# A four-layer graph network on one core: 8 more node blocks gathered in the first pass, two weights joined, casts and one-hots on other engines, 40 instead of 36 blocks by weight matrix

## The chip, the cores and the metric

The kernel runs on one core of one Trainium2 chip. The metric is device time in microseconds: the median of the runs before the change is 8338.6 us (three runs, 8333.83 to 8340.75).

The core has five engines with a queue each, which work through their instructions in order: PE (matmuls; PEld is its loading of weights, which overlaps), DVE (vectors), ACT (scalar functions, copies, casts), POOL (general purpose; here it issues the gathers) and SP (issues most of the plain DMAs). SBUF is the memory on the chip, PSUM holds PE's results.

## The reference

Four layers over one graph of 12,500 nodes with 64 features and 212,500 directed edges (sorted by destination). Each adds its result to x and normalizes each row:

```python
msgs = x[src]                                              # layer 0, SAGE, twice
mean = segment_sum(msgs, dst) / maximum(deg, 1)
h = relu(mean @ Wl.T + bl + x @ Wr.T)
h = relu(h @ W1.T + b1) @ W2.T + b2
out = sage(h)                                              # conv2_Wl, conv2_bl, conv2_Wr
msg = silu(batchnorm(concat(x[row], edge_attr) @ W1 + b1)) # layer 1, summed by node
out = segment_sum((feat @ weight + h_bias)[src] * attention, dst)    # layer 2
for _ in range(3):                                         # layer 3
    h = segment_sum(norm[:, None] * h[src], dst)
```

## The kernel before

Nodes lie in 98 blocks of 128. Edges lie in 1664 groups of up to 128, 8 groups to a chunk (208 chunks). A sum over the edges of a node block is formed in one of two ways.

**Gathered** (`gather_pass`): for each group POOL fetches 128 source rows with one indirect DMA (line 382, tile `msg`), DVE makes a one-hot of the destinations (line 297, `oh` or `ohs`), and PE multiplies one with the other into the block's PSUM tile `ps` (line 334). A group touches one to three blocks. Precision comes from cutting f32 into three bf16 parts side by side (`split`, lines 279 to 285): ACT casts `hi`, DVE takes the rest, ACT casts `mid`, DVE takes `lo`. POOL, DVE, ACT and PE each come in turn.

**By matrix**: the block's rows of the adjacency matrix times all 98 blocks of sources, with no gathering.

The work runs in six stages:

1. *First pass* (about 190 to 1460 us of the profile). `adjacency` (line 586) builds the fp8 adjacency of blocks 28 to 97 from windows of 4 nodes: one-hots of keys (DVE, line 608) and sources (DVE, line 601), a product `pb` (PE, line 613), a cast to fp8 (ACT, line 617), and a write of each block to DRAM (`t_adj`, line 626). As each is finished, its product with the node features, `px` (line 790, 98 matmuls), is spread over the building of the next. Beside it the first 496 groups are gathered from `t_x` for blocks 0 to 29. Blocks 28 and 29 get a share of both, kept in `shares` and added. Each finished sum goes through `conv1` (line 715): mean, three 64-wide layers one after another (line 722), then a product with the second convolution's two weights (line 726), splits, and writes to `t_h` and `t_hs`. `together` deals the steps of the two sides evenly.
2. *Second pass* (to 2204 us): blocks 30 to 97 with `t_adj` read back in halves (`at`, line 354, 4 buffers; `pd`, line 359), the first 496 groups gathered from `t_h`.
3. *Edge rows* (2214 to 4300 us): all 1664 groups are gathered from `t_y`, added to the edges' own product (`pe`, lines 871 and 872), copied (`h`, line 874) and written with the one-hots to DRAM. Beside it `weight_matrix` (line 677) builds the attention-weighted adjacency of the last 36 blocks in f32: for each window of 4 nodes a `wkeys` one-hot (DVE, line 690), three weighted one-hots `wlows` (DVE, line 694, one for each bf16 part of the weights), three matmuls `pw` (line 697), a copy `aw` (ACT, line 698), and a write of four windows (SP, line 700).
4. *Silu sums* (4300 to 4840 us): per chunk, ACT applies silu to the rows read back (`z`, line 911), PE transposes (`pm`), `split_messages` makes the bf16 parts, and the stored one-hots are read for the product `ps`. Messages are made two chunks ahead. `update` follows for each block.
5. *Weighted sums* (4952 to 6301 us): the last 36 blocks by the stored f32 matrix (`by_matrix`, line 1036: 7 loads of 0.9 MB and 196 matmuls `pdw`, line 1044, per block), the others from 1064 groups gathered from `t_a`, scaled by ACT (line 1034). A `Later` queue delays the steps that follow a block (transposes, products, table writes) by so many pieces of the matrix.
6. *Three hops* (6331 us to the end), each like the second pass, over `t_g`.

In stages 1 to 4 and 6 a scheduler sets the order of instructions within each queue; in stage 5 it is the program's own order for ACT, DVE and PE.

Of the kernel before, what the change touches and what calls it, by code (L numbers as in the profile page):

```python
# [32 lines left out]

NW = 36
W = 128
# [24 lines left out]
def static_windows(n_nodes, n_edges):  # L60


    last = -(-n_nodes // P) * P - 1
    out = []
    for e, n in edge_groups(n_edges):
        margin = LEAST + int(MARGIN * 2 * (e * (n_edges - e)) ** 0.5 / n_edges)
        lo = e * n_nodes // n_edges - margin
        hi = (e + n) * n_nodes // n_edges + margin
        lo, hi = min(max(lo, 0), last), min(max(hi, 0), last)
        if n < P:  # L70
            hi = last
        out.append((lo // P, hi // P - lo // P + 1))
    return out


# [173 lines left out]
def fast(ctx: ExitStack, net: Net):  # L249
# [9 lines left out]
    bmax = max(b0 + n - 1 for b0, n in wins[:G0])  # L259
    dmin = min(b0 for b0, _ in wins[G0:])  # L260
    HB = NB // 2
    assert NB % 2 == 0 and G0 % J == 0 and dmin <= bmax + 1 and all(n <= 2 for _, n in wins[:G0])

# [14 lines left out]

    def split(parts, t, rest):

        hi, mid, lo = parts
        nc.scalar.copy(hi, t)
        nc.vector.tensor_tensor(rest, t, hi, ALU.subtract)  # L283
        nc.scalar.copy(mid, rest)  # L284
        nc.vector.tensor_tensor(lo, rest, mid, ALU.subtract)
# [111 lines left out]

    def split_messages(work, t, bufs=4):
# [3 lines left out]
        split(thirds(msg), t, rest)  # L402
        return msg
# [21 lines left out]

    def transposed(t):

        m = t.shape[1]
        pt = psum.tile([P, P], F32, name="pxt", tag="a")
        nc.tensor.transpose(pt[0:m, :], t, ident)  # L430
        xt = node.tile([P, P], F32, name="xt")
        nc.scalar.copy(xt[0:m, :], pt[0:m, :])
        return xt[0:m, :]
# [152 lines left out]
    def adjacency(block):  # L586
# [3 lines left out]
        with tc.tile_pool(name="build", bufs=1) as build:  # L590
            for b in range(dmin, NB):
                w0, w1 = b * P // D, min((b + 1) * P // D, n_win)
# [83 lines left out]

    def weight_matrix(kw, wkey, wlow, parts, ramps):

        kramp, lramp = ramps
        for b in range(B0, NB):  # L680
            w0 = b * PW
            for w in range(w0, w0 + PW, 4):
                n = max(0, min(4, n_win - w))
                aw = kw.tile([P, 7, 4, CS], F32, name="aw", bufs=3)
                if n < 4:
                    nc.vector.memset(aw, 0.0)
                for i in range(n):
                    k = w + i - QB * RW
                    keys = kw.tile([P, KEYS], BF16, name="wkeys", bufs=4)
# [14 lines left out]
                yield  # L704
# [8 lines left out]
    t_hs = dram.tile([P, NB, T3], BF16, name="t_hs")  # L713

    def conv1(b, ps):
        nc.vector.tensor_single_scalar(rdeg[:, b : b + 1], ps[:, T3 : T3 + 1], CU, ALU.max)
        nc.vector.reciprocal(rdeg[:, b : b + 1], rdeg[:, b : b + 1])  # L717
        nc.vector.tensor_single_scalar(dinv2[:, b : b + 1], ps[:, T3 : T3 + 1], CU, ALU.add)
        h = transposed(mean_and_own(b, ps))
        for weight, bias, func in ((net.w1, BL1, AF.Relu), (wt[:, M1, :], BM1, AF.Relu), (wt[:, M2, :], BM2, AF.Identity)):  # L720
            p1 = psum.tile([F, P], F32, name="p1", tag="a")
            nc.tensor.matmul(p1, weight, h, start=True, stop=True)  # L722
            h = node.tile([F, P], F32, name="h1")
            nc.scalar.activation(h, p1, func, bias=col[0:F, bias : bias + 1])
# [23 lines left out]
    with tc.tile_pool(name="xs0", bufs=1) as xp:  # L748
        xx = xp.tile([P, NB, XW], BF16, name="xx")
        with (  # L750
# [31 lines left out]


            shares = kl.tile([P, bmax - dmin + 1, T3 + 1], F32, name="shares")
            shared = set()

            def block(b, a):
                pd = psum.tile([P, T3 + 1], F32, name="px")
                for s in range(NB):
                    nc.tensor.matmul(pd, a[:, s, :], xx[:, s, 0 : T3 + 1], start=s == 0, stop=s == NB - 1)  # L790
                    if s % 7 == 6:
                        yield
                if b > bmax:
                    conv1(b, pd)
                else:
                    nc.scalar.copy(shares[:, b - dmin, :], pd)
                    shared.add(b)

            def gathered_block(b, ps):
                if b >= dmin:  # L800
                    assert b in shared
                    both = node.tile([P, T3 + 1], F32, name="both")
                    nc.vector.tensor_tensor(both, ps[:, 0 : T3 + 1], shares[:, b - dmin, :], ALU.add)
                    ps = both
                conv1(b, ps)
# [98 lines left out]
    with tc.tile_pool(name="keep1", bufs=1) as keep1, tc.tile_pool(name="work2s", bufs=2) as work:  # L904
        hT = keep1.tile([F, NP], F32, name="hT")

        def silu_message(c):
# [94 lines left out]

    GW = -(-(1 + max(g for g, (b0, _) in enumerate(wins) if b0 < B0)) // J) * J
    with tc.tile_pool(name="xs3", bufs=1) as xp:
        xs = xp.tile([P, NB, T3], BF16, name="xs")

        def weighted_sum(b, total):
# [13 lines left out]

            later3.add(3, columns)

        later3 = Later()

        with tc.tile_pool(name="work3", bufs=1) as work, tc.tile_pool(name="adj3", bufs=4) as adj:
# [10 lines left out]
            def by_matrix():  # L1037
                for b in range(B0, NB):
# [14 lines left out]
                    def to_rows(b=b, sums_t=sums_t):  # L1053
                        pt = psum.tile([P, F], F32, name="pxw", tag="c", bufs=2)
                        nc.tensor.transpose(pt, sums_t, i64)
                        weighted_sum(b, pt)

                    later3.add(2, to_rows)

# [442 lines left out]
```

## Time and profile before

| what | us |
|---|---|
| median of three runs | 8338.6 |
| the profiled execution | 8331.0 |
| its span, first to last instruction | 8329.2 |
| PE busy | 7023.3 (84%) |
| POOL busy | 5140.4 (62%) |
| DVE busy | 4699.4 (56%) |
| ACT busy | 3293.7 (40%) |

Busy shares are means over six stages with different limits, so each stage has to be read by itself. A profile line of a group gives the source line, the engine, the operation, output<-input, shapes and count, then its busy time, the mean length of one in ns, and the idle time before it with what ended it. A line of waits gives who waited for whom: us in total, times, longest. A line of the timeline gives start, length, engine, line, operation. "issue" is time in which an engine waited for nothing that the profile shows.

### The profile page before, as it was taken

The page shows a single profiled execution, that of the slowest core. Times are in us where ns is not written, and L with a number is a line of the kernel's source. Part 1 is how long each engine was busy: PE and PEld are TensorE (multiplying, and loading weights), DVE is VectorE, ACT ScalarE, POOL GpSimd, SP SyncE. Part 2 cuts the span into 40 slices and gives each one's busy share as a digit, 9 for nine tenths or more (in the row PEclk, how much of TensorE's full clock was granted, in tenths as well). Part 3 has the DMA queues.
Part 4 walks back from the last instruction along what each step waited for, and adds up shares of the span by engine and source line. Part 5 has one row for each costly group of instructions (what it writes and reads, how often), then busy time and mean ns, then how long its engine had stood idle before and what let it go on. Part 6 is the DMA issues. An engine that isn't in the chain of part 4 may idle for free.

```text
span 8329.2 us, 168327 instructions
## 1 busy us (share of the span) xinstructions
PE 7023.3 (84%) x63175; PEld 5984.5 (72%) x63176; DVE 4699.4 (56%) x16465; ACT 3293.7 (40%) x7517; POOL 5140.4 (62%) x5281
## 2 busy tenths in 40 slices
PE   1999999999866666666768877888889999999999
PEld 0777777899744444444447767777778999999999
DVE  7999998333478999998976642222222232322333
ACT  5888888111123333333348854444442111111110
POOL 4644442777477777777740017777776776776775
PEclk9999999899888888888879968999999999999999
DMA  4433333666567788877789946777776776776676
GB/s 103 137 114 120 122 113 113 196 206 197 173 218 246 250 257 261 262 252 247 251 268 328 327 152 243 250 254 263 267 268 215 217 217 211 217 217 213 211 219 183
DMA packets 863605, 1786.57 MB, mean 214 GB/s; under 512 B 250245, under 2 KB 511904, under 8 KB 853695
## 3 DMA queue, kind: packets, MB, share of 16 engines
q1 hardware_dynamic: 629944, 1382.63, 49.2%
q0 software_dynamic: 171856, 216.73, 11.1%
q10 hardware_dynamic: 60980, 176.35, 5.7%
q8 instruction: 501, 8.21, 0.4%
q14 instruction: 324, 2.65, 0.1%
HBM read 1217.67 MB, written 557.45 MB: 213 GB/s over the span
## 4 chain that ended last, share of the span: by engine, by line
PE 42%; POOL 24%; DMA 13%; issue 11%; DVE 6%; ACT 4%; POOLq 0%; ACTq 0%; DVEq 0%; SPq 0%
POOL msg L382 24%; PE pd L359 15%; DMA msg<-t_y,srci 8%; PE px L790 7%; PE pb L613 4%; PE ps L334 4%; DMA msg<-t_a,srci 3%; PE pw L697 3%; DMA msg<-t_g,srci 2%; PE p L722 1%; PE pe L872 1%; DVE rest L283 1%; ACT parts L284 1%; DVE junk L511 1%; PE ps L359 1%
## 5 line engine op out<-in xcount | busy, mean ns | idle before, releaser
L359 PEld LDWEIGHTS <-at 128*128 128x128 fp8e4 x27440 | 2280.0, 98 | 21.0 <-issue 15.5
L359 PE MATMUL pd<-xs,at 128*128 128x192 bf16 x26656 | 2264.5, 247 | 2.8 <-DMA at<-t_adj 2.8
L382 POOL DMA_INDIRECT msg<-t_y,srci x1664 | 1570.1, 944 | 582.1 <-issue 442.5
L382 POOL DMA_INDIRECT msg<-t_g,srci x1488 | 1406.8, 945 | 567.9 <-issue 453.8
L382 POOL DMA_INDIRECT msg<-t_a,srci x1064 | 1025.0, 963 | 985.8 <-DMA t_a<-xa 661.7
L697 PE MATMUL pw<-wkeys,wlows 128*128 128x392 bf16 x3423 | 1012.8, 389 | 172.8 <-ACT h L874 102.5
L694 DVE TENSOR_SCALAR wlows<-wramp,wlow,wpart 128x132 bf16<-128x132 f16 x3423 | 975.0, 334 | 231.8 <-PE pw L697 223.9
L378 DVE TENSOR_REDUCE sum<-pd 128x64 f32<-128x192 f32 x272 | 97.3, 358 | 1765.1 <-PE pd L362 1235.8
L698 ACT COPY aw<-pw 128x392 f32<-128x392 f32 x1141 | 554.6, 486 | 1224.2 <-PE pw L697 1209.0
L617 ACT ACTIVATE a<-pb 128x784 fp8e4<-128x784 f32 x1115 | 916.9, 825 | 156.2 <-PE pb L613 99.1
L382 POOL DMA_INDIRECT msg<-t_x,srci x496 | 563.8, 1137 | 608.1 <-PE pb L613 280.6
L1044 PE MATMUL pdw<-atw,xa 128*64 128x128 f32 x7056 | 879.5, 286 | 7.5 <-issue 7.5
L872 PE MATMUL pe<-ident,msg 128*128 128x128 f32 x1664 | 424.8, 344 | 508.2 <-DMA msg<-t_y,srci 505.8
L1044 PEld LDWEIGHTS pdw<-atw,xa 128*64 128x64 f32 x7056 | 822.6, 144 | 40.9 <-issue 32.7
L872 PEld LDWEIGHTS pe<-ident,msg 128*128 128x128 f32 x1664 | 337.2, 235 | 635.9 <-issue 463.5
L790 PE MATMUL px<-xx,a 128*128 128x193 bf16 x6860 | 779.0, 248 | 1.6 <-DVE rdeg L717 0.7
L297 DVE TENSOR_SCALAR oh<-ramp,drel 128x258 bf16<-128x258 f16 x2480 | 740.7, 338 | 6.5 <-PE ps L334 5.8
L697 PEld LDWEIGHTS <-wlows 128*128 128x128 bf16 x3423 | 382.8, 112 | 468.6 <-DVE wlows L694 371.4
L790 PEld LDWEIGHTS <-a 128*128 128x128 fp8e4 x6860 | 582.8, 98 | 159.9 <-issue 45.9
L608 DVE TENSOR_SCALAR keys<-line,key 128x392 bf16<-128x392 f16 x2229 | 625.6, 326 | 93.9 <-PE pb L613 83.6
L613 PE MATMUL pb<-keys,lows 128*128 128x392 bf16 x2229 | 571.2, 330 | 7.9 <-ACT a L617 3.4
L382 POOL DMA_INDIRECT msg<-t_h,srci x496 | 469.0, 945 | 169.4 <-issue 137.4
(233 smaller groups left out, 8978.0 us busy)
## 6 DMA issues: line engine op xcount, KB each, us to landing
at<-t_adj SPq DMA_DIRECT2D x560, 784.0 KB
t_w<-aw SPq DMA_DIRECT2D x288, 784.0 KB
atw<-t_w SPq DMA_DIRECT2D x252, 896.0 KB
ohs<-t_oh SPq DMA_DIRECT2D x279, 516.0 KB
t_adj<-a SPq DMA_DIRECT2D x70, 1568.0 KB
t_oh<-ohs ACTq DMA_DIRECT2D x176, 516.0 KB
ec<-in_ea SPq DMA_DIRECT2D x208, 256.0 KB
t_e<-h ACTq DMA_DIRECT2D x208, 256.0 KB
```

Of the source, the lines that this page charges most:

```text
L297: nc.vector.tensor_scalar(oh[:, 0 : 3 * ramp.shape[2]], ramp, net.drel[:, g : g + 1], one, ALU.is_equal, ALU.mult)
L359: nc.tensor.matmul(ps[:, 0:T3], at[:, s, :], xs[:, h * HB + s, :], start=start, stop=left == 0)
L382: nc.gpsimd.indirect_dma_start(out=out, out_offset=None, in_=table, in_offset=bass.IndirectOffsetOnAxis(ap=net.srci[:, g : g + 1], axis=0),)
L608: nc.vector.tensor_scalar(keys, net.line[:, 0:KEYS], key[:, w - Q0 * RW : w - Q0 * RW + 1], CU, ALU.is_equal, ALU.mult)
L613: nc.tensor.matmul(pb[:, i % 2, 0:KEYS], lows[:, i, :], keys, start=True, stop=True)
L617: nc.scalar.activation(a[:, :, at : at + k * D].rearrange("p s (k d) -> p k s d", d=D), pb[:, 0:k, 0:KEYS].rearrange("p k (s d) -> p k s d ...
L694: nc.vector.tensor_scalar(lows, lramp, wlow[:, k : k + 1], parts[j][:, k : k + 1], ALU.is_equal, ALU.mult)
L697: nc.tensor.matmul(pw, lows[:, 0:P], keys, start=j == 0, stop=j == 2)
L698: nc.scalar.copy(aw[:, :, i, :], pw.rearrange("p (a c) -> p a c", a=7))
L790: nc.tensor.matmul(pd, a[:, s, :], xx[:, s, 0 : T3 + 1], start=s == 0, stop=s == NB - 1)
L872: nc.tensor.matmul(pe[:, at], both, ident, start=False, stop=True)
L1044: nc.tensor.matmul(pd, xa[:, a * (NB // 7) + s, :], at[:, :, s * D : (s + 1) * D], start=a == 0 and s == 0, stop=a == 6 and s == NB // 7 - 1,)
```

## The change

- First pass: blocks 28 to 35 are now gathered whole (624 groups, `GA`, instead of 496; `below=BA` cuts off what falls into later blocks). `shares` goes. Their adjacency is still built, for the later passes, but with no `px`; the build order is 36, 37, 38, 39, 28, 40 to 45, 29, and so on, one of the eight after every six.
- The MLP's last weight has no nonlinearity behind it: `join_weights` multiplies it once with the next convolution's two weights (`m2lr`), and its bias likewise (`blr`, on all partitions). `conv1` has two 64-wide layers, one product, and one add `rr`.
- Second pass: 5 buffers of `at` instead of 4. `aw`, `wkeys` and `wlows` move from the pool `kw`, open in stages 2 and 3, to the pool of stage 3.
- Weight matrix: 40 blocks instead of 36. DVE makes the one-hot for part 0 as before and a bare one (`low1`); ACT makes those of parts 1 and 2 by scaling it.
- Silu sums: the cast of `mid` is a copy on POOL instead of ACT.
- Weighted sums: 1000 groups gathered; delays of 4 in two places (3 and 2 before); two PSUM tags exchanged.

```diff
-NW = 36
+NW = 40
...
+def chunks_below(wins, b):
+
+    return -(-(1 + max(g for g, (b0, _) in enumerate(wins) if b0 < b)) // J) * J
...
+    BA = dmin + J
+    GA = chunks_below(wins, BA)
+    build_order = []
+    for b in range(BA, NB):
+        build_order.append(b)
+        if b - BA >= 3 and (b - BA - 3) % 6 == 0 and dmin + (b - BA - 3) // 6 < BA:
+            build_order.append(dmin + (b - BA - 3) // 6)
...
-    def split(parts, t, rest):
+    def split(parts, t, rest, second=nc.scalar.copy):
...
-        nc.scalar.copy(mid, rest)
+        second(mid, rest)
...
-    def transposed(t):
+    def transposed(t, tag="a", bufs=None):
...
-            for b in range(dmin, NB):
+            for b in build_order:
...
                     pw = psum.tile([P, KEYS], F32, name="pw", tag="agg", bufs=3)
+                    low1 = work.tile([P, 132], BF16, name="wlow1", bufs=4)
+                    nc.vector.tensor_single_scalar(low1, lramp, wlow[:, k : k + 1], ALU.is_equal)
                     for j in range(3):
-                        lows = kw.tile([P, 132], BF16, name="wlows", bufs=8)
-                        nc.vector.tensor_scalar(
-                            lows, lramp, wlow[:, k : k + 1], parts[j][:, k : k + 1], ALU.is_equal, ALU.mult
-                        )
+                        lows = work.tile([P, 132], BF16, name="wlows", bufs=8)
+                        if j == 0:
+                            nc.vector.tensor_scalar(
+                                lows, lramp, wlow[:, k : k + 1], parts[j][:, k : k + 1], ALU.is_equal, ALU.mult
+                            )
+                        else:
+                            nc.scalar.activation(lows, low1, AF.Copy, scale=parts[j][:, k : k + 1])
                         nc.tensor.matmul(pw, lows[:, 0:P], keys, start=j == 0, stop=j == 2)
...
+    def join_weights():
+        pt = psum.tile([P, P], F32, name="pxt", tag="a")
+        nc.tensor.transpose(pt[0:F, 0:F], wt[:, M2, :], i64)
+        m2t = node.tile([F, P], F32, name="h1")
+        nc.scalar.copy(m2t[:, 0:F], pt[0:F, 0:F])
+        pm = psum.tile([P, 2 * F], F32, name="pr2", tag="a")
+        nc.tensor.matmul(pm[0:F, :], m2t[:, 0:F], net.wlr2, start=True, stop=True)
+        nc.scalar.copy(m2lr, pm[0:F, :])
+        same = node.tile([F, P], F32, name="h1")
+        nc.vector.tensor_copy(same, col[0:F, BM2 : BM2 + 1].to_broadcast([F, P]))
+        pm = psum.tile([P, 2 * F], F32, name="pr2", tag="a")
+        nc.tensor.matmul(pm, same, net.wlr2, start=True, stop=True)
+        nc.scalar.copy(blr, pm)
+        nc.vector.tensor_tensor(blr[:, F : 2 * F], blr[:, F : 2 * F], row[:, RL2, :], ALU.add)
...
-        for weight, bias, func in ((net.w1, BL1, AF.Relu), (wt[:, M1, :], BM1, AF.Relu), (wt[:, M2, :], BM2, AF.Identity)):
+        for weight, bias in ((net.w1, BL1), (wt[:, M1, :], BM1)):
...
-        nc.tensor.matmul(pr, h, net.wlr2, start=True, stop=True)
+        nc.tensor.matmul(pr, h, m2lr, start=True, stop=True)
+        rr = node.tile([P, 2 * F], F32, name="rr")
+        nc.vector.tensor_tensor(rr, pr, blr, ALU.add)
...
-        split(thirds(hp), pr[:, 0:F], rest)
+        split(thirds(hp), rr[:, 0:F], rest)
...
-        nc.vector.tensor_tensor(X[:, b, :], X[:, b, :], pr[:, F : 2 * F], ALU.add)
-        nc.vector.tensor_tensor(X[:, b, :], X[:, b, :], row[:, RL2, :], ALU.add)
+        nc.vector.tensor_tensor(X[:, b, :], X[:, b, :], rr[:, F : 2 * F], ALU.add)
...
             def block(b, a):
+                if b < BA:
+                    return
...
-            sums = gather_pass(work, G0, gathered(work, t_x, XW), gathered_block, m=T3 + 1, open_blocks=2)
-            together(sums, G0 // J, adjacency(block), n_build)
+            sums = gather_pass(work, GA, gathered(work, t_x, XW), conv1, m=T3 + 1, open_blocks=2, below=BA)
+            together(sums, GA // J, adjacency(block), n_build)
...
-            tc.tile_pool(name="adj1", bufs=4) as adj,
+            tc.tile_pool(name="adj1", bufs=5) as adj,
...
-            together(edge_rows(work, stats), NCH - J, weight_matrix(kw, *weights), n_weight)
+            together(edge_rows(work, stats), NCH - J, weight_matrix(work, *weights), n_weight)
...
-            return split_messages(work, pm.rearrange("p (j f) -> p j f", j=J))
+            return split_messages(work, pm.rearrange("p (j f) -> p j f", j=J), second=nc.gpsimd.tensor_copy)
...
-                xt = transposed(X[:, b, :])
+                xt = transposed(X[:, b, :], "c", 2)
...
-            later3.add(3, columns)
+            later3.add(4, columns)
...
-                        pt = psum.tile([P, F], F32, name="pxw", tag="c", bufs=2)
+                        pt = psum.tile([P, F], F32, name="pxw", tag="a")
...
-                    later3.add(2, to_rows)
+                    later3.add(4, to_rows)
```

More of the change, by code (lines that the diff above doesn't have):

```diff
@@ L260, in fast @@
     dmin = min(b0 for b0, _ in wins[G0:])
+    BA = dmin + J
[5 more added lines that the diff above has]
+            build_order.append(dmin + (b - BA - 3) // 6)
     HB = NB // 2
+    assert bmax < BA and sorted(build_order) == list(range(dmin, NB))
     assert NB % 2 == 0 and G0 % J == 0 and dmin <= bmax + 1 and all(n <= 2 for _, n in wins[:G0])
@@ L396, in gathered, with split_messages @@
         return message
-    def split_messages(work, t, bufs=4):
+    def split_messages(work, t, bufs=4, second=nc.scalar.copy):
         msg = work.tile([P, J, T3], BF16, name="parts", bufs=bufs)
         rest = work.tile([P, J, F], F32, name="rest", bufs=2)
-        split(thirds(msg), t, rest)
+        split(thirds(msg), t, rest, second)
         return msg
@@ L424, in layernorm @@
         nc.scalar.activation(X[:, b, :], X[:, b, :], AF.Identity, bias=shift, scale=sd)
-    def transposed(t):
+    def transposed(t, tag="a", bufs=None):
         m = t.shape[1]
-        pt = psum.tile([P, P], F32, name="pxt", tag="a")
+        pt = psum.tile([P, P], F32, name="pxt", tag=tag, bufs=bufs)
         nc.tensor.transpose(pt[0:m, :], t, ident)
@@ L675, in spread_weights, with weight_matrix @@
         return wkey, wlow, parts, ramps
-    def weight_matrix(kw, wkey, wlow, parts, ramps):
+    def weight_matrix(work, wkey, wlow, parts, ramps):
         kramp, lramp = ramps
@@ L683, in weight_matrix @@
                 n = max(0, min(4, n_win - w))
-                aw = kw.tile([P, 7, 4, CS], F32, name="aw", bufs=3)
+                aw = work.tile([P, 7, 4, CS], F32, name="aw", bufs=3)
                 if n < 4:
@@ L688, in weight_matrix @@
                     k = w + i - QB * RW
-                    keys = kw.tile([P, KEYS], BF16, name="wkeys", bufs=4)
+                    keys = work.tile([P, KEYS], BF16, name="wkeys", bufs=4)
                     nc.vector.tensor_scalar(keys, kramp, wkey[:, k : k + 1], None, ALU.is_equal)
                     pw = psum.tile([P, KEYS], F32, name="pw", tag="agg", bufs=3)
+                    low1 = work.tile([P, 132], BF16, name="wlow1", bufs=4)
+                    nc.vector.tensor_single_scalar(low1, lramp, wlow[:, k : k + 1], ALU.is_equal)
                     for j in range(3):
-                        lows = kw.tile([P, 132], BF16, name="wlows", bufs=8)
-                        nc.vector.tensor_scalar(
-                            lows, lramp, wlow[:, k : k + 1], parts[j][:, k : k + 1], ALU.is_equal, ALU.mult
-                        )
+                        lows = work.tile([P, 132], BF16, name="wlows", bufs=8)
[5 more added lines that the diff above has]
+                            nc.scalar.activation(lows, low1, AF.Copy, scale=parts[j][:, k : k + 1])
                         nc.tensor.matmul(pw, lows[:, 0:P], keys, start=j == 0, stop=j == 2)
@@ L713, in fast @@
     t_hs = dram.tile([P, NB, T3], BF16, name="t_hs")
+    m2lr = keep.tile([F, 2 * F], F32, name="m2lr")
+    blr = keep.tile([P, 2 * F], F32, name="blr")
+    def join_weights():
[12 more added lines that the diff above has]
+        nc.vector.tensor_tensor(blr[:, F : 2 * F], blr[:, F : 2 * F], row[:, RL2, :], ALU.add)
     def conv1(b, ps):
@@ L723, in conv1 @@
             h = node.tile([F, P], F32, name="h1")
-            nc.scalar.activation(h, p1, func, bias=col[0:F, bias : bias + 1])
+            nc.scalar.activation(h, p1, AF.Relu, bias=col[0:F, bias : bias + 1])
         pr = psum.tile([P, 2 * F], F32, name="pr2", tag="a")
-        nc.tensor.matmul(pr, h, net.wlr2, start=True, stop=True)
+        nc.tensor.matmul(pr, h, m2lr, start=True, stop=True)
+        rr = node.tile([P, 2 * F], F32, name="rr")
+        nc.vector.tensor_tensor(rr, pr, blr, ALU.add)
         rest = node.tile([P, F], F32, name="nrest")
         hp = node.tile([P, T3], BF16, name="hp")
-        split(thirds(hp), pr[:, 0:F], rest)
+        split(thirds(hp), rr[:, 0:F], rest)
         nc.sync.dma_start(t_h[b * P : (b + 1) * P, :], hp)
         nc.sync.dma_start(t_hs[:, b, :], hp)
-        nc.vector.tensor_tensor(X[:, b, :], X[:, b, :], pr[:, F : 2 * F], ALU.add)
-        nc.vector.tensor_tensor(X[:, b, :], X[:, b, :], row[:, RL2, :], ALU.add)
+        nc.vector.tensor_tensor(X[:, b, :], X[:, b, :], rr[:, F : 2 * F], ALU.add)
     def parts_of_x(prep, b0):
@@ L781, in fast @@
             nc.sync.dma_start(t_wlow, low[:, (QB - Q0) * RW :])
-            shares = kl.tile([P, bmax - dmin + 1, T3 + 1], F32, name="shares")
-            shared = set()
+            join_weights()
             def block(b, a):
+                if b < BA:
+                    return
                 pd = psum.tile([P, T3 + 1], F32, name="px")
@@ L792, in block @@
                         yield
[L793 to L805, printed above, removed]
-            sums = gather_pass(work, G0, gathered(work, t_x, XW), gathered_block, m=T3 + 1, open_blocks=2)
-            together(sums, G0 // J, adjacency(block), n_build)
+                conv1(b, pd)
+            sums = gather_pass(work, GA, gathered(work, t_x, XW), conv1, m=T3 + 1, open_blocks=2, below=BA)
+            together(sums, GA // J, adjacency(block), n_build)
     psum = ctx.enter_context(tc.tile_pool(name="psum1", bufs=1, space=PSUM))
@@ L1001, in fast @@
     t_g = table("t_g0")
-    GW = -(-(1 + max(g for g, (b0, _) in enumerate(wins) if b0 < B0)) // J) * J
+    GW = chunks_below(wins, B0)
     with tc.tile_pool(name="xs3", bufs=1) as xp:
```

## The prediction

> **What bounds the kernel now.** First I read the busy time, cut where the kind of work changes. Columns: busy time and instruction count of PE, PEld, DVE, ACT and POOL, then granted PE clock, DMA share, GB/s.
>
> ```profile
> 190.00:1460.00 1270.00, 1252.70 (x10824) 935.67 (x10823) 1126.47 (x3772) 1056.15 (x1896) 563.75 (x496) 1.00 0.35 120
> ...
> 1518.00:2204.00 686.00, 682.04 (x7811) 653.19 (x7809) 237.05 (x1169) 98.79 (x293) 455.55 (x482) 1.00 0.65 197
> ...
> 2214.00:4300.00 2086.00, 1396.88 (x6730) 929.92 (x6729) 1815.42 (x6401) 667.92 (x1344) 1569.69 (x1664) 0.84 0.77 246
> 4300.00:4840.00 540.00, 451.97 (x4227) 373.36 (x4227) 337.94 (x627) 472.99 (x1021) 0.00 (x0) 0.98 0.92 321
> ...
> 4952.00:6301.00 1349.00, 1112.15 (x9258) 1024.33 (x9257) 348.56 (x1078) 591.71 (x1830) 1024.68 (x1064) 0.91 0.73 258
> ...
> 6331.00:8329.00 1998.00, 1945.47 (x23387) 1932.01 (x23384) 608.10 (x2757) 228.37 (x784) 1406.38 (x1488) 1.00 0.69 212
> ```
>
> So there are six stages with different limits. The second (second SAGE sum) and the sixth (three hops) are PE nearly all the time, and the change alters none of their PE work. For the other four I read the chain and the waits.
>
> First stage: the chain cut to 190 to 1460 us is 94.3% PE (px 47.5%, pb 28.8, p 8.3, ps 5.1, pr 3.1, pxt 1.5), but DVE is busy 89% and ACT 83% beside it.
>
> Third and fifth: POOL's waits for 2214 to 4290 us and for 4952 to 6301 us begin with
>
> ```profile
> POOL msg L382 <- issue: 442.5, 1452, 0.3
> ...
> POOL msg L382 <- issue: 301.8, 990, 0.3
> ```
>
> 0.30 us of issue each time and nothing longer: gathers run back to back, 0.94 + 0.30 = 1.25 us each. 1664 of them are 2076 us, the third stage; 1064 took 4952.3 to 6300.4, 1.268 us each, the fifth. PE's waits in the fifth, on ACT copies queued behind scalings that wait for gathered rows, follow from that:
>
> ```profile
> PE pxw L1055 <- ACT sums_t L1051: 90.9, 22, 10.7
> PE pxt L430 <- ACT xt L432: 90.4, 26, 8.9
> PE pxt L430 <- ACT X L424: 33.5, 14, 5.5
> ```
>
> Fourth: POOL idle, no single full engine. A piece of its timeline:
>
> ```profile
> 4506.50 0.69 DVE L283 TENSOR_TENSOR rest<-pm,parts 128x512 f32<-128x512 f32 x1 [1.35 <-ACT parts L282]
> ...
> 4507.88 0.69 DVE L285 TENSOR_TENSOR parts<-rest,parts 128x512 bf16<-128x512 f32 x1 [0.69 <-ACT parts L284]
> ...
> 4509.60 0.62 ACT L284 CAST parts<-rest 128x512 bf16<-128x512 f32 x1 [0.76 <-DVE rest L283]
> 4510.12 0.81 ACT L911 ACTIVATE z<-h,sb 128x512 f32<-128x512 f32 x1
> ```
>
> DVE takes chunks in turn: rest, wait for the middle cast, lo, next rest. ACT makes that cast, and the next silu (z) stands behind it. 208 chunks take about 527 us (4305 to 4832), 2.53 us each.
>
> **First pass.** Removed: 784 px matmuls (98 for each of 8 blocks). The chain has 7 px in 0.59 us, 0.084 each: 66 us of PE. One of three L722 layers per block: 98 x 0.36 (two passes) = 35 us of PE, and 98 x 0.354 = 35 us of ACT. Added: 128 gathers, 231 ps matmuls x 0.084 = 19 us, and 128 one-hots of 0.338 us, 43 us of DVE. The bias add becomes a 128x128 add from PSUM; between the rows 0.209 (128x64) and 0.413 (128x256) I take 0.28, and one 0.216 add goes: +0.065 x 98 = 6 us of DVE. The eight copies and adds of shares go (about 2 us on each of ACT and DVE). The 128 gathers cost 128 x 1.44 = 184 us of POOL, which waited 608 us in this stage: hidden, and beyond that cover they would be paid in full. Joining the weights is three small PE products ahead of the window transposes, where PE waited 133 us: nothing, at most the 3 us of its chain of copies. The same 70 t_adj writes and 196 writes of t_h and t_hs go out on SP in another order; nobody waits for them before the stage ends.
>
> PE: 66 + 35 - 19 = 82 us less. DVE: 1126 + 43 + 6 - 2 = 1173 us. If PE stayed the bound the stage would take 1270 - 82 = 1188 us, and DVE would be 98.7% full; no engine is that full in any stage but those of plain PE work. Ends: -82, and 0 (DVE with the slack it has now would need 1173 / 0.89 = 1318 us, more than today; I cap that at today, since its slack now is waiting for PE). In blocks 28 to 35 PE has no px to do, so part of the relief falls where DVE paces anyway. I take DVE at 95%: 1235 us, **-35 us**.
>
> **Second pass.** A fifth adjacency buffer: the page shows 2.8 us of waiting for such a load in all four passes. **0**.
>
> **Third stage.** Each of 1269 windows (1141 before) loses two lows on DVE (0.285 each, 975 / 3423) and gains one bare one-hot, taken at the same: DVE 1815 - 1141 x 0.285 + 128 x (0.406 + 0.57) = 1615 us. ACT gains 2538 scaled copies of 128x132. Bounds: the 128x64 scaled row alone is 0.340 and eight in a row take 2.00, 0.25 each; 68 more elements at 0.833 ns (from the 64- and 512-wide casts, 243 and 616 ns) add 0.057: 0.307 to 0.397 us, 779 to 1008 us. With 128 more aw copies (0.486, 62 us), and 416 DMA issues of 0.33 us that ACT's busy time leaves out (137 us), ACT stands at 668 + 62 + 137 + 779 to 1008 = 1646 to 1875 of 2086 us, below POOL's 2076. 384 more pw matmuls x 0.389 = 149 us at most on a PE with 690 us idle. 32 more t_w writes on SP. POOL is untouched: **0**, and the 200 us taken from DVE buy nothing. Aw, keys and lows move into a pool that opens after the second stage, so the few windows now made early start with the stage: a few us, within the range.
>
> **Fourth stage.** In the built order DVE still has rest, lo, rest, lo, with lo now waiting for POOL; queued behind it are the sums (cat on ACT, pxt on PE, wait for them) and the next rest, and ps waits for lo. The loop is 0.69 + x + 0.69, 0.05 of hand-off, and 0.15 of the sum and statistics (0.35 + 0.28, 98 times in 208, half within the wait): 1.58 + x. ACT drops out: z no longer queues behind the cast. No POOL cast is in the trace. Bounds: the write-only IOTA of 512 elements, 0.544; the TENSOR_SCALAR rows of 1700 elements, 4.56 to 5.94 us, less 0.11 of start, scaled to 512: 1.45 to 1.87. Between them, the fastest TENSOR_TENSOR (3.06 us, two inputs): 0.11 + 512 x 1.73 ns = 1.00. It is a plain f32 read and write as the cast is, so I take it: 2.58 us a chunk, 208 x 0.05 = **+10 us**. Ends: at 0.54 PE holds at about 2.4 us (two chunks in the tightest stretch, 4689.8 to 4694.7, took 4.90 with PE hardly pausing), -27; at 1.87, 208 x 0.92 = +191.
>
> The Trainium skill speaks against this step: GPSIMD Engine Reference, section 3, calls that engine the wrong choice for ordinary elementwise arithmetic. Its 769 ns for 512 elements in the tightest loop would, as an estimate, put the stage at PE's floor, -27 us instead of +10.
> SBUF — State Buffer, "Who interferes with whom", lets a DVE instruction with two SBUF inputs and a reading GpSimd instruction exclude each other. The trace agrees: a DVE cast of 128x128 took 2.61 us beside POOL arithmetic. Overlap would cost up to x a chunk, 208 us; the order forbids it, since lo waits for its own POOL cast and the next cast waits for the next rest.
>
> **Fifth stage.** 64 gathers x 1.268 = 81 us of POOL go, with 64 scalings (ACT, 22 us) and 140 ps matmuls (12 us of PE). Four more blocks by matrix: 4 x 24.4 (879.5 / 36) = 98 us of PE, and 28 more 0.9 MB loads through SP; at 258 GB/s now and 325 in the fourth stage they fit. PE's busy time becomes 1112 + 98 - 12 = 1198 of 1268 us, 94%, if its 237 us of waits shrink to 70. They can: they follow POOL's pace, and the delays of 4 steps (from 2 and 3) give each ACT copy two more pieces of PE work as cover. Ends: -81, and 1198 + 237 - 1349 = +86 if every wait stays. I take the POOL end less 11 us for a tighter PE: **-70 us**. The 30 us between last t_a and first t_g gather stay.
>
> **Sum**: -35 + 0 + 0 + 10 - 70 = -95 us on the profiled execution (8331.0 us, span 8329.2), 8236. The median of the three runs, 8338.6, lies 7.6 above it, so I predict **8243.6 us**.
>
> **Rivals.**
> 1. Dear POOL cast (slower): DVE waits for POOL in the fourth stage. For: POOL's one-input rows, 2.6 to 3.4 ns an element. Against: they convert int32, and some ran while DVE held them up. At their mean, x = 1.66: 208 x (3.24 - 2.53) = +148 for +10, 8382 us. It decides from x = 1.46, where the stage's loss eats the other 105. Chance 0.25.
> 2. ACT binds in the third stage: 1875 us plus 0.2 us of hand-off for each of 1269 windows is 2129, 53 over POOL: 8297 us. For: PE waits 363 us for rows in 2400 to 4000 us, with pw behind it and aw behind that. Against: a slower chain finds its rows landed. 0.12.
> 3. Everything at its good end, -82 - 27 - 81 = -190: 8149 us. Against: DVE 98.7% full. 0.12.
> 4. Fifth stage only half freed: half of PE's waits stay, 1198 + 119 = 1317, -32 for -70: 8282 us. 0.09.
>
> **Numbers.** My forecast has 0.42. The range 8165 to 8385 us leaves out the far ends of rivals 3 and 1, under 2 in 10. A step of 0.2% (17 us) is what a measurement of this kernel can tell from none. Faster: 0.42 + 0.03 + 0.08 + 0.12 + 0.07 = 0.72; within 0.2%: 0.05 + 0.03 + 0.02 = 0.10; slower: 0.17 + 0.01 = 0.18.
>
> **What would show it.** First stage shorter by 20 to 50 us with DVE above 93%; third unchanged, POOL's issue waits still 0.3 us and DVE near 77%; fourth: the POOL cast's own row and DVE waiting for it, 2.5 to 2.6 us a chunk; fifth: 1000 gathers, 1.27 us each, PE's waits for sums_t and xt far below 181 us. I am wrong if the cast takes over 1.4 us, if POOL waits on PE or ACT in the third stage, or if PE's waits in the fifth stay.

## The result, and the profile after

| | before | after |
|---|---|---|
| median of four runs, us | 8336.4 (8333.8 to 8340.8) | 8216.9 (8211.2 to 8219.0) |
| the profiled execution, us | 8331.0 | 8217.3 |
| its span, us | 8329.2 | 8215.6 |

The ratio of after to before is 0.9855, with a 95% interval of 0.9838 to 0.9872: 119.5 us less by the medians, 113.7 by the profiled executions. The forecast was 8243.6 us in a range of 8165 to 8385.

The busy time of the changed kernel, cut where its stages change. Columns as before: busy time and count of PE, PEld, DVE, ACT and POOL, granted PE clock, DMA share, GB/s.

```profile
190.00:1430.00 1240.00, 1185.75 (x10077) 875.36 (x10076) 1151.75 (x3893) 1030.41 (x1795) 715.57 (x624) 0.99 0.38 125
1430.00:1488.00 58.00, 16.20 (x47) 6.45 (x47) 9.69 (x42) 8.88 (x33) 40.75 (x36) 0.55 0.67 208
1488.00:2199.60 711.60, 704.25 (x8019) 672.90 (x8018) 242.85 (x1193) 105.07 (x306) 458.69 (x486) 0.99 0.64 194
2199.60:4277.00 2077.40, 1438.00 (x7122) 787.35 (x7120) 1611.84 (x5658) 1448.66 (x4010) 1570.04 (x1664) 0.90 0.81 260
4293.00:4793.00 500.00, 452.91 (x4187) 369.77 (x4188) 323.19 (x604) 362.79 (x797) 127.75 (x207) 0.99 0.96 345
...
4917.40:6193.90 1276.50, 1151.05 (x9965) 1067.64 (x9964) 334.89 (x1053) 564.61 (x1751) 971.62 (x1000) 0.96 0.80 287
```

Boundaries set by eye move by some us, so for the balance I cut both traces at the same events: the first and last instruction on one tile or table.

| from, to | before, us | after, us | change | predicted |
|---|---|---|---|---|
| first px, last px (first pass) | 1255.2 | 1226.1 | -29.1 | -35 |
| last px, first t_y gather (second pass) | 754.7 | 769.8 | +15.1 | 0 |
| first, last t_y gather (third stage) | 2076.0 | 2076.0 | 0.0 | 0 |
| first, last silu z (fourth) | 520.1 | 498.5 | -21.6 | +10 |
| first, last t_a gather (fifth) | 1348.1 | 1275.2 | -72.9 | -70 |
| last t_a, first t_g gather | 30.2 | 28.3 | -1.9 | 0 |
| first t_g gather, end (hops) | 1998.6 | 1994.7 | -3.9 | 0 |

With the two short gaps beside the fourth stage (+0.1 and +0.6) this adds up to -113.6, the difference of the spans. The hops have the same work on both sides; in four more runs below they took 1995 to 2004 us, so -3.9 lies within their scatter.

So two rows are as forecast for the whole stage (third, fifth), the first is near, and two are off: the second pass lost 15 us that were not foreseen, and the silu stage gained 22 us where a loss of 10 was expected.

**Third and fifth.** POOL's waits for 2200 to 4276 us, and then for 4917 to 6194 us:

```profile
POOL msg L397 <- issue: 470.3, 1543, 0.3
```

```profile
POOL msg L397 <- issue: 285.7, 937, 0.3
```

Still 0.30 us each and nothing longer: the gathers run back to back in both. What PE waited for in the fifth stage:

```profile
PE pr L1045 <- ACT xt L447: 43.3, 15, 7.4
PE pxt L445 <- ACT X L439: 33.8, 16, 8.6
PE pdw L1072 <- DMA atw<-t_w: 31.1, 30, 3.7
```

The waits for sums_t are gone, 125 us of 237 remain, and a new one is there: PE now waits 30 times, 31.1 us in all, for the stored matrix.

**Fourth.** A piece of the timeline of the changed kernel (start, length, engine, line):

```profile
4504.81 0.69 DVE L298 TENSOR_TENSOR rest<-pm,parts 128x512 f32<-128x512 f32 x1 [1.30 <-ACT parts L297]
4504.93 0.80 ACT L939 ACTIVATE z<-h,sb 128x512 f32<-128x512 f32 x1
...
4505.63 0.61 POOL L299 CAST parts<-rest 128x512 bf16<-128x512 f32 x1 [2.85 <-DVE rest L298]
...
4506.28 0.69 DVE L300 TENSOR_TENSOR parts<-rest,parts 128x512 bf16<-128x512 f32 x1 [0.59 <-POOL parts L299]
```

POOL's cast takes 0.61 us, as ACT's did, and the next silu z starts on ACT while DVE still makes rest. Before, it stood behind the cast. A chunk takes 498.5 / 207 = 2.41 us instead of 2.51, and PE is busy 91% of the stage. DVE waits for the middle cast as long as before (134.2 us, 128.4 before); what fell are PE's waits for z, from 55.0 to 37.0 us.

**Second pass.** What PE did for the product pd in the 60 us after the last px, before and after (PE's and DVE's busy time with count, clock, DMA share, GB/s):

```profile
1458.90:1518.90 60.00, 31.98 (x202) 0.72 (x2) 0.63 0.58 176
```

```profile
1429.80:1489.80 60.00, 2.42 (x16) 0.00 (x0) 0.55 0.65 202
```

202 of the second pass's products against 16. Before, PE's timeline has them between the small transposes pwt, from ahead of the first one on:

```profile
1465.94 1.28 PE L359 MATMUL pd<-xs,at 128*128 128x192 bf16 x7
1467.46 0.44 PE L657 MATMUL pwt<-ident,wsome 125*128 125x125 f32 x1 [0.24 <-DMA wsome<-in_eatt,wat]
1467.69 0.84 PE L359 MATMUL pd<-xs,at 128*128 128x192 bf16 x4
```

PE's timeline of the changed kernel shows what stood in the way:

```profile
1482.54 0.44 PE L672 MATMUL pwt<-ident,wsome 125*128 125x125 f32 x1 [1.49 <-DMA wsome<-in_eatt,wat]
1484.06 0.44 PE L672 MATMUL pwt<-ident,wsome 125*128 125x125 f32 x1 [1.08 <-DMA wsome<-in_eatt,wat]
1484.55 0.32 PE L349 MATMUL ps<-msg,oh 128*128 128x192 bf16 x1
1486.76 0.44 PE L672 MATMUL pwt<-ident,wsome 125*128 125x125 f32 x1 [1.89 <-DMA wsome<-in_eatt,wat]
1487.27 0.32 PE L349 MATMUL ps<-msg,oh 128*128 128x192 bf16 x1
1487.38 7.82 PE L374 MATMUL pd<-xs,at 128*128 128x192 bf16 x76
```

20 of the 25 small transposes pwt wait for their gather of edge weights, and pd comes in PE's queue behind the last one.

The Trainium skill bears on these 58 us (TensorE: Matmul & The Clock Gate, Part 1): an idle PE falls back to half its clock after a few us without work. The trace fits that: PE was busy 16.2 us of the 58, with gaps of up to 3.8 us, and 0.55 of full speed was granted, against 0.99 on either side.

### The profile page after: what moved, and what is told of

Same layout as the page of the kernel before. It is cut to its first block, busy times and chain, and to the rows that moved or that the text cites. A ratio compares the mean times of both kernels' runs of the same rounds, so it can differ in the third digit from the quotient of the medians.

```text
span 8215.6 us, 170270 instructions
## 1 busy us (share of the span) xinstructions
PE 7031.1 (86%) x63463; PEld 5814.4 (71%) x63464; DVE 4505.7 (55%) x15816; ACT 3922.5 (48%) x9802; POOL 5367.2 (65%) x5553
## 4 chain that ended last, share of the span: by engine, by line
PE 41%; POOL 22%; issue 12%; DMA 12%; DVE 10%; ACT 3%; ACTq 0%; DVEq 0%; POOLq 0%; SPq 0%
POOL msg L397 22%; PE pd L374 17%; PE px L830 6%; PE ps L349 5%; PE pb L628 4%; DMA t_oh<-ohs 3%; DMA msg<-t_a,srci 3%; PE pw L717 2%; DMA msg<-t_y,srci 2%; DMA msg<-t_g,srci 2%; DVE ohs L312 2%; DVE wlows L712 1%; DVE wkeys L705 1%; PE pm L942 1%; DVE keys L623 1%
## 5 line engine op out<-in xcount | busy, mean ns | idle before, releaser
L397 POOL DMA_INDIRECT msg<-t_a,srci x1000 | 971.6, 972 | 426.5 <-issue 285.7
L397 POOL DMA_INDIRECT msg<-t_x,srci x624 | 715.6, 1147 | 456.0 <-PE pb L628 241.4
L1072 PE MATMUL pdw<-atw,xa 128*64 128x128 f32 x7840 | 938.0, 280 | 38.7 <-DMA atw<-t_w 31.1
L1072 PEld LDWEIGHTS pdw<-atw,xa 128*64 128x64 f32 x7840 | 880.6, 140 | 72.7 <-DMA atw<-t_w 38.5
L716 ACT ACTIVATE wlows<-wlow,wpart 128x132 bf16<-128x132 bf16 x2538 | 878.7, 400 | 21.2 <-DMA ec<-in_ea 0.8
L718 ACT COPY aw<-pw 128x392 f32<-128x392 f32 x1269 | 611.2, 482 | 553.2 <-PE pw L717 545.2
L830 PE MATMUL px<-xx,a 128*128 128x193 bf16 x6076 | 684.5, 248 | 3.2 <-ACT a L632 2.4
L312 DVE TENSOR_SCALAR ohs<-ramp,drel 128x258 bf16<-128x258 f16 (+1 forms) x1664 | 536.3, 350 | 172.7 <-DMA t_oh<-ohs 171.4
L830 PEld LDWEIGHTS <-a 128*128 128x128 fp8e4 x6076 | 524.5, 98 | 141.9 <-issue 29.7
L705 DVE TENSOR_SCALAR wkeys<-wramp,wkey 128x392 bf16<-128x392 f16 x1269 | 520.9, 410 | 146.4 <-PE pw L717 134.1
```

What stands on the lines that cost most here:

```text
L312: nc.vector.tensor_scalar(oh[:, 0 : 3 * ramp.shape[2]], ramp, net.drel[:, g : g + 1], one, ALU.is_equal, ALU.mult)
L397: nc.gpsimd.indirect_dma_start(out=out, out_offset=None, in_=table, in_offset=bass.IndirectOffsetOnAxis(ap=net.srci[:, g : g + 1], axis=0),)
L716: nc.scalar.activation(lows, low1, AF.Copy, scale=parts[j][:, k : k + 1])
L1072: nc.tensor.matmul(pd, xa[:, a * (NB // 7) + s, :], at[:, :, s * D : (s + 1) * D], start=a == 0 and s == 0, stop=a == 6 and s == NB // 7 - 1,)
```

## The experiments

Each kernel ran beside the kernel before, on the same chip. The chips were not alike: on two of them (the first four runs and the last four) PE was held back, and every kernel, the one before included, took 11.2 to 11.6 ms; a section at the end shows how. From those runs only what does not depend on PE's speed, or what differs between two kernels far beyond the scatter, is read.

**1. ACT casts the middle part again.**

```diff
-            return split_messages(work, pm.rearrange("p (j f) -> p j f", j=J), second=nc.gpsimd.tensor_copy)
+            return split_messages(work, pm.rearrange("p (j f) -> p j f", j=J))
```

> The changed kernel with one edit undone: in the silu stage ACT casts the middle part again. Theory (the loop of DVE is 1.39 us of its own work plus the wait for the cast, and with the cast on POOL the next silu no longer stands behind it on ACT): the stage goes back from 2.41 to 2.51 us a chunk, 208 x 0.10 = +21 us, 8238 us, and PE waits again for silu rows. Rival (the stage gained from the other edits, not from the cast): 2.41 us a chunk stays, 8217 us. The other stages: no change by either.

Measured: 11310.7 us, ratio to before 0.9973 (0.9954 to 0.9993). The silu stage isn't held back on this chip (granted clock 0.99). From first to last z, with the cast on ACT (this run) and on POOL (run 3, same chip):

```profile
5499.80:6021.10 521.30, 446.78 (x4182) 370.13 (x4183) 326.55 (x602) 462.94 (x1000) 0.00 (x0) 0.99 0.94 331
```

```profile
5466.40:5967.10 500.70, 453.02 (x4182) 370.15 (x4183) 321.82 (x602) 360.94 (x794) 127.34 (x206) 0.99 0.96 344
```

521.3 against 500.7 us, 2.52 against 2.42 a chunk. In the fourteen traces of this case the three kernels with ACT's cast take 520 to 522 us and the eleven with POOL's 498 to 502, whatever else they change. The theory holds: the cast alone is worth 21 us. That it helps in ACT's queue, and not in DVE's loop, fits the waits shown above.

**2. Not joined** (and again as 8, at the full clock).

```diff
-        for weight, bias in ((net.w1, BL1), (wt[:, M1, :], BM1)):
+        for weight, bias, func in ((net.w1, BL1, AF.Relu), (wt[:, M1, :], BM1, AF.Relu), (wt[:, M2, :], BM2, AF.Identity)):
...
-        nc.tensor.matmul(pr, h, m2lr, start=True, stop=True)
+        nc.tensor.matmul(pr, h, net.wlr2, start=True, stop=True)
```

> The changed kernel with three 64-wide layers and two bias adds in the first pass again, nothing joined; the 8 blocks are still gathered. PE and ACT get back 98 x 0.36 = 35 us each, DVE loses about 6. Theory (in the first pass PE at 96% and DVE at 93% pace by turns): about half of it shows, +15 to +25 us in the first pass, 8232 to 8242 us. Rival A (DVE alone paces): 0 or -6, 8211 to 8217 us. Rival B (PE alone paces): +35, 8252 us.

Measured: 11344.5 us, ratio 0.9990 (0.9967 to 1.0013); first to last px 1578 us against 1533 in run 1, whose first pass is that of the change. See 8.

**3. Two blocks more instead of eight** (and again as 7).

```diff
-    BA = dmin + J
+    BA = dmin + 2
```

> The changed kernel with 2 blocks more gathered whole in the first pass instead of 8 (520 groups instead of 624): PE gets 588 px back and loses some 190 small products, 588 x 0.084 - 190 x 0.084 = +33 us; DVE loses 104 one-hots, 104 x 0.34 = -35 us. Theory (PE and DVE pace by turns): the two nearly cancel, -5 to +15 us, 8212 to 8232 us. Rival A (PE alone paces): +33, 8250 us. Rival B (DVE alone paces): -35, 8182 us.

Measured: 11243.7 us, ratio 0.9904 (0.9867 to 0.9941); first to last px 1502 us, 31 less than in run 1. See 7.

**4. Of the change, only the move of aw, wkeys and wlows to another pool.**

```diff
-            together(edge_rows(work, stats), NCH - J, weight_matrix(kw, *weights), n_weight)
+            together(edge_rows(work, stats), NCH - J, weight_matrix(work, *weights), n_weight)
```

> The kernel before with one edit of the change alone: the tiles aw, wkeys and wlows come from the pool that opens with the third stage. In the trace of the change PE did none of the second pass's products while the 25 small gathers of edge weights came in; in the trace of before it did 196 there. Theory (moving these tiles changes the order that the scheduler writes for PE, weight transposes ahead of the products): 196 products come later, 196 x 0.084 = 16 us, first t_y gather 10 to 16 us later after the same first pass, 8336 + 13 = 8349 us. Rival (the products wait for their loads whatever the order): no change, 8336 us.

Measured: 11368.7 us, ratio 1.0017 (0.9997 to 1.0036), which by itself doesn't tell 13 us from none. The trace does tell the mechanism, since the order in PE's queue doesn't depend on the chip. pd in the 60 us after the last px of this kernel:

```profile
1776.50:1836.50 60.00, 4.83 (x29) 0.00 (x0) 0.52 0.62 189
```

29 products instead of 202, and the first of them, at 1829.39 us, stands behind 24 of the 25 transposes, with nothing changed but the pool that three tiles come from. So this edit turns the order of PE's queue. Its price at the full clock was not measured alone; run 5 repairs the order in another way and gives 14 us.

**5. The small gathers, transposes and copies dealt out between dense blocks.** `spread_weights` becomes a generator that stops after each gather; `hybrid_pass` takes a step of it before each dense block from the third on.

```diff
             for b in range(bmax + 1, NB):
+                if b > bmax + 2:
+                    next(side, None)
                 ps = psum.tile([P, T3], F32, name="pd", tag="blk", bufs=2)
```

> The changed kernel, with the 25 small gathers of edge weights, their transposes (pwt) and copies dealt out one by one between the dense blocks of the second pass, instead of standing ahead of it. In the trace of the change PE does 16 us of work in the 58 us after the last px, and the first t_y gather comes 770 us after the last px (755 before the change). Theory (the products pd stand behind the transposes in PE's queue, and those wait for POOL's gathers): PE starts on pd about 8 us after the last px and is slowed only until the 14 loads of xs and the first loads of the matrix have landed, some 25 us; 740 to 750 us to the first t_y gather, -20 to -30 us, about 8192 us. Rival A (the loads hold the products as long): 765 to 770 us, 8217 us. Rival B (the gathers of t_h are held up between the small ones and the 496 groups become late): over 770 us, slower.

Measured: 8207.4 us, ratio 0.9840 (0.9824 to 0.9857). Last px to first t_y gather 755.7 us, 14 less than in the changed kernel and 1 more than before the change. pd in the 60 us after the last px:

```profile
1437.70:1497.70 60.00, 19.27 (x219) 0.71 (x2) 0.69 0.74 242
```

219 products again. The theory holds in kind; it expected 740 to 750 us. The remainder has the same shape: PE's first pd now stands behind products of gathered rows (ps), for which PE waits 22 us.

**6. 36 blocks by weight matrix, the rest as changed.**

```diff
-NW = 40
+NW = 36
```

> The changed kernel with 36 blocks by weight matrix instead of 40; the delays, tags and one-hots on ACT stay. Theory (POOL's gathers pace stages three and five): the third stage takes the same 2076 us from first to last gather, though DVE, ACT and PE have a tenth less to do for the matrix; the fifth takes 1063 x 1.27 = 1350 us instead of 1275, +75 us, 8292 us. Rival (the fifth stage gained by the delays and tags, which took PE's waits away): under +40 us in the fifth, below 8257 us.

Measured: 8310.1 us, ratio 0.9962 (0.9948 to 0.9976). The gathers of the fifth stage, of this run and of the changed kernel (count, shortest, median and longest in ns, first and last start):

```profile
L397 POOL DMA_INDIRECT msg<-t_a,srci x1064: 940/945/1452, 4930.5 to 6283.1; - x178
```

```profile
L397 POOL DMA_INDIRECT msg<-t_a,srci x1000: 940/944/1454, 4917.4 to 6192.6; - x167
```

1352.6 us against 1275.2: the four blocks are worth 77 us there. Against 1348.1 before the change, with the short delays and the same 1064 gathers, the new delays and tags are worth nothing at 36 blocks. PE's waits in the stage were moved and not lessened: 236 us in this run, as before the change, none of them for sums_t but 130 for xt. The third stage took 2077.8 us, as long with 128 windows less. Both belong to the theory that POOL paces. (The profiled execution is 100 us longer than that of the change, not 77. The other 22 lie in stages with the same work, 9.5 of them in the hops and 4.7 ahead of the first px. The median too is 93 us longer, so it is not this one execution; the cause isn't shown.)

**7. Two blocks more, at the full clock.**

> The changed kernel with 2 blocks more gathered whole in the first pass instead of 8 (520 groups instead of 624), as before but to be read at the full clock. PE gets 33 us of work more, DVE 35 less. Theory (PE at 96% and DVE at 93% pace by turns): first to last px product 1215 to 1240 us instead of 1226, 8207 to 8231 us. Rival A (PE alone paces): +33, 8250 us. Rival B (DVE alone paces): -35, 8182 us.

Measured: 8212.2 us, ratio 0.9845 (0.9828 to 0.9861).

**8. Not joined, at the full clock.**

> The changed kernel with three 64-wide layers in the first pass and two bias adds, nothing joined, to be read at the full clock. PE and ACT get 35 us of work each, DVE loses about 6. Theory (PE and DVE pace by turns): first to last px product 1241 to 1251 us instead of 1226, 8232 to 8242 us. Rival A (DVE alone paces): 1220 to 1226 us, 8211 to 8217 us. Rival B (PE alone paces, or ACT's layers lie in its way too): 1260 us or more, 8252 us.

Measured: 8259.9 us, ratio 0.9902 (0.9885 to 0.9918). First to last px of the changed kernel, of 7 and of 8:

```profile
203.70:1429.80 1226.10, 1176.29 (x10046) 872.04 (x10043) 1139.35 (x3860) 1017.78 (x1778) 709.76 (x619) 0.99 0.38 126
```

```profile
210.70:1420.80 1210.10, 1194.01 (x10429) 908.67 (x10427) 1118.51 (x3754) 1020.65 (x1777) 577.26 (x514) 0.99 0.37 122
```

```profile
206.50:1470.30 1263.80, 1219.09 (x10239) 885.05 (x10237) 1135.71 (x3858) 1037.27 (x1875) 698.91 (x620) 0.99 0.38 122
```

Without the join (8) the pass takes 38 us more, which is rival B's size there (PE alone), and 9 more than before the change. With fewer blocks gathered (7) it takes 16 us less, 1210.1, though PE has 18 us more to do: between the theory and that run's rival B (DVE alone). (The whole of run 7 is only 5 us below the changed kernel, on another chip, so by the time alone the two can't be told apart. The stage can: the unaltered first pass of the change took 1226.5 and 1228.5 us in runs 5 and 6.)

So no single pace explains both. PE idles 16 us in run 7 and 50 in the changed kernel. PE's waits for keys from 400 to 1200 us, in the changed kernel and in run 7:

```profile
PE pb L628 <- DVE keys L623: 13.1, 26, 1.0
```

```profile
PE pb L628 <- DVE keys L623: 1.9, 4, 0.6
```

For the cast of pb it waits 7.6 us there, and 1.9 in run 7. Over the whole pass its waits for gathered rows differ too: 16.8 us in the changed kernel, 7.9 in run 7. So PE loses by waiting more than the 18 us of products that it was spared. The keys fit an account in which gathering puts more one-hots between them on a DVE that is 92% busy already; no run separates this from the rows that come later. The join takes 43 us of work from PE and 20 from ACT, and hardly any of that is lost again.

**9. The delays and tags of before, with 40 blocks.**

```diff
-            later3.add(4, columns)
+            later3.add(3, columns)
...
-                    later3.add(4, to_rows)
+                    later3.add(2, to_rows)
```

> The changed kernel with the delays of 3 and 2 and the PSUM tags of before in the fifth stage; 40 blocks stay. Theory (PE, 90% busy there now, keeps up with POOL only because the longer delays took away its waits for ACT's copies, 237 us before, 129 now): PE's waits for sums_t and xt come back and the stage, first to last gather, takes 1295 to 1335 us instead of 1275, 8237 to 8277 us. Rival (POOL's gathers pace it either way, and the waits only fill PE's slack): 1270 to 1285 us, 8217 to 8227 us.

Measured: 11523.5 us, ratio 1.0036 (1.0022 to 1.0051), on a chip that holds PE back. The fifth stage took 1918 us, and 1889 in run 10 on the same chip with the long delays; runs 1 to 3, which have the same fifth stage, took 1846 to 1875. Inconclusive: the difference is as large as that scatter.

**10. All one-hots by DVE, 40 blocks.**

```diff
-                        else:
-                            nc.scalar.activation(lows, low1, AF.Copy, scale=parts[j][:, k : k + 1])
```

> The changed kernel with all three one-hots of a window made by DVE again, none by ACT; 40 blocks stay. DVE has 1612 - 347 + 2534 x 0.285 = 1987 us in a third stage of 2076 us, 96%. Theory (DVE's relief was needed for 40 blocks, as an engine that is 96% full no longer follows POOL's pace): the third stage takes 2090 to 2150 us from first to last gather, 8231 to 8291 us. Rival (POOL paces up to the brim, the one-hots on ACT buy nothing): 2076 us, 8217 us.

Measured: 11409.7 us, ratio 0.9935 (0.9918 to 0.9951). The third stage took 2489 us; with ACT's one-hots (runs 9, 11, 12 on that chip) 2566 to 2611. On such a chip ACT's one-hots cost time. What paces the stage there isn't settled: PE is busy 1522 us and pauses for no recorded cause for another 275, and it waits 288 us for wlows and 143 for ACT's copy h. Whether DVE, with the 1948 us of work that this trace shows, would hold a stage of 2076 us at the full clock isn't answered.

**11 and 12. Joined up: two blocks, the dealt-out gathers, and 41 or 44 blocks by matrix.**

```diff
-NW = 40
+NW = 41
```

> A version from the results so far: the changed kernel with 2 blocks more gathered in the first pass instead of 8, the small gathers of edge weights dealt out between the dense blocks of the second pass, and 41 blocks by weight matrix (984 groups gathered). Theory (the three add up, as they lie in three stages): first pass 1210 us and 755 to the first t_y gather as in those runs, fifth stage 983 x 1.276 = 1254 us instead of 1275; 8217 - 9 - 14 - 20 = 8174 us. Rival (PE, with 1151 + 24 - 4 = 1171 us in the fifth stage, no longer follows): 1275 us there, 8194 us.

> The version with 2 blocks in the first pass and the dealt-out small gathers, with 44 blocks by weight matrix instead of 41 (928 groups gathered; the stored matrix lies in two tensors). Theory (past some 41 blocks PE paces the fifth stage): PE has 1151 + 98 - 12 = 1237 us there and keeps waits of 50 us or more, 1280 to 1320 us from first to last gather or to the last product, against 927 x 1.276 = 1183 us for POOL; with the third stage still 2076 us the time is 8200 to 8240 us, slower than with 41. Rival (POOL still paces): 1183 to 1200 us in the fifth stage, 8100 to 8120 us.

Measured: 11463.5 us, ratio 0.9989 (0.9974 to 1.0003), and 11484.2 us, 1.0011 (0.9994 to 1.0027). The fifth stage took 1923 and 1926 us, and PE paced it: in run 11 its busy time (1375 us) and its pauses without a releaser (543) fill it. Neither expectation can be judged on that chip. The best version at the full clock is run 5, 8207.4 us; its interval overlaps that of the change, and its lead (9.5 us by the medians) is read in the stage that it alters, 14 us there.

## Why the prediction was right or wrong, step by step

- **First pass, -35, measured -29.1.** Right in sum, wrong in its parts. I put PE's relief at 82 us, 47 of it from gathering and 35 from the join. PE's busy time fell by 67 (1243.6 to 1176.3 from first to last px), 43 of it by the join (run 8). The step that failed is "PE: 66 + 35 - 19": run 8 has 784 px less than before and some 231 ps more, and PE is busy only 25 us less, so a ps costs 0.18 us if px holds at 0.084, and not 0.084. That they cost more because they stand scattered between others is not shown. And what gathering took from PE came back as waiting for DVE's keys, ACT's casts and gathered rows. The sum came near by luck: it was 1173 us of DVE at 95%, and the stage had 1152 us at 93%, two errors that cancel. The join gave 38 us; gathering eight blocks whole, in place of the shares, cost 9 (run 8 against before).
- **Second pass, 0, measured +15.** The fifth buffer is indeed worth nothing to see: all waits of pd for at fell from 2.8 us to 0.2. The failed step is the last sentence on the third stage, that aw, keys and lows "move into a pool that opens after the second stage", with "a few us" for the early windows. The cost lay elsewhere: the move turned PE's order (run 4), and 186 products of 0.084 us, 16 us, went from a time in which PE waits to one in which it is full. Run 5 gives 14 us back.
- **Third stage, 0, measured 0.0.** DVE had 1612 us (1615 predicted), ACT 1449 and its 416 issues of 0.33, 1586 (1646 to 1875 predicted; its scaled copies took 0.400 us each, just above my upper bound, but neighbours overlap in the records: 2534 of them are busy 877 us together). POOL paced, and run 6 with fewer windows took no less. That DVE's relief buys nothing even with 40 blocks is not shown.
- **Fourth stage, +10, measured -21.6.** The mechanism was right on ACT's side, where z no longer stands behind the cast; the size of one term was wrong: x = 1.00 us for POOL's cast, measured 0.613. The loop of DVE is then 1.58 + 0.61 = 2.19, below the 2.4 that I had read as PE's floor, and the stage stops at 2.41, near the good end (-27). So DVE's loop, which the forecast let pace the stage, doesn't. Nor is 2.4 shown to be a floor: PE is busy 453 of the 500 us. I had chosen the two-input arithmetic row; the same cast on ACT, 0.616 us, would have been the closer neighbour. The Trainium skill (GPSIMD Engine Reference, section 3.1) has 769 ns for 512 elements in its tightest loop; this cast was faster, so here the measurement decides. Its advice to use DVE for elementwise work was not put to the test: the cast came from ACT, and POOL, idle in that stage before, took it in the same time. The exclusion of DVE and POOL that the prediction weighed did not show: DVE's two steps took 0.69 us each, as before.
- **Fifth stage, -70, measured -72.9.** Right, POOL paces it at 1.276 us a gather. PE was busy 1151 us, not 1198: its products pdw, which were to cost 98 us more, took 868 us in the stage before and 931 after, under a granted clock of 0.91 and 0.96. PE kept 125 us of waits where 70 were foreseen. That the longer delays make this possible was only argued: run 6 shows them worth nothing at 36 blocks, and run 9 couldn't decide for 40.
- **The rivals.** The dear POOL cast and ACT as the bound are refuted by rows (0.613 us; 2076.0 us), the half-freed fifth stage by -72.9. Of "everything at its good end" the fourth and fifth nearly came about; the first pass and PE's order kept it from -190. The errors by stage (+6, +15, -32, -3, and -6 of scatter in the last rows) add up to only -19 us, and the 7.6 us that I allowed between the profiled execution and the median did not come back (8217.3 and 8216.9). That 8243.6 lies only 27 us from 8216.9 is luck in part: +15 and -32 are errors of separate stages that offset each other.

## What to carry to other kernels

Where two engines are both nearly full, take work out of the pass altogether (the join) before moving it from the fuller to the less full: here, what PE was spared by gathering came back as waits for the engines that got the work. An edit that only moves tiles between pools can change the order a scheduler writes for another engine; look at what stands in its queue around the boundary between stages, behind instructions that wait for loads. For an operation that the trace doesn't show on one engine, look at the same operation on another engine too: here it was the closer neighbour (0.616 us for 0.613), though one case makes no rule.

## What the runs showed of the hardware

On the two chips with the long times PE isn't evenly slower. In the hops of the changed kernel PE waits for nearly nothing: it is busy 1945 of 1994 us. Its waits in the hops of run 3 (8500 to 11000 us) begin with

```profile
PE pd L374 <- issue: 528.8, 842, 3.2
```

842 pauses, the longest 3.2 us, for which no releaser is recorded. Cut into pieces of 4 us (busy time and count of PE, PEld, DVE, ACT, POOL, then the granted clock, DMA share, GB/s):

```profile
9000.00:9004.00 4.00, 4.00 (x51) 4.00 (x49) 0.43 (x2) 0.00 (x0) 3.08 (x4) 1.00 0.51 161
9004.00:9008.00 4.00, 2.30 (x23) 1.54 (x20) 0.00 (x0) 0.00 (x0) 3.09 (x4) 1.00 0.19 38
9008.00:9012.00 4.00, 2.14 (x13) 1.52 (x14) 0.00 (x0) 0.00 (x0) 1.04 (x2) 0.59 0.70 221
9012.00:9016.00 4.00, 4.00 (x30) 3.82 (x28) 2.21 (x9) 1.22 (x5) 0.00 (x0) 0.55 0.40 100
9016.00:9020.00 4.00, 4.00 (x52) 4.00 (x50) 1.21 (x7) 0.24 (x1) 0.00 (x0) 1.00 0.37 134
```

First 51 products in 4 us at the full clock, then pauses with 23 and 13 products, with the clock falling to little over half, then full speed again. The hops took 3247 us instead of 1995, the silu stage hardly more (500.7 against 498.5), and two rows of other engines kept their durations (in run 1, ACT's scaled copies 401 ns and POOL's gathers of t_y 943, against 400 and 944). What pauses PE there is shown by no trace, and the change's own gain on such a chip wasn't measured.
